# A block read by an adding transfer freed at a later slot, and a chunk's small factors moved down the order, in a three-layer cross-interaction kernel

## The chip, the cores and the metric

The kernel runs on one core of one Trainium2 chip. The metric is the device time of one launch in microseconds (us). The kernel before was timed in three runs; a fourth execution was profiled.

## The reference, cut to what matters

The input `r_x` has 1024 batch items, 64 features and 16 embedding columns, in f32. Three layers follow each other. Each multiplies all pairs of features of the input with the features of the running state, and contracts the pairs with a weight matrix of 128 rows:

```
x0 = h = x                                  # (1024, 64, 16)
for i in range(3):
    z = einsum('bfe,bge->bfge', x0, h)      # all pairs of features
    y = einsum('oc,bce->boe', W[i], z) + b[i]
    x_i, h = (y[:, :64], y[:, 64:]) if i < 2 else (y, y)
    xs.append(x_i)
out = sum(concatenate(xs, axis=1), axis=2) @ fc_w.T + fc_b     # (1024, 1)
```

Only one number per batch item leaves, so the kernel folds the last layer's weights and the output vector into the weights of the layers before, ahead of the main part.

## The kernel before, in words

**Tiling.** The 1024 items are cut into 32 chunks of 32 items; a chunk has 32 x 16 = 512 columns. The products of pairs of features of one chunk fill 16 tiles of 128 rows by 512 columns. Four tiles make a block (128 x 2048, f32, 1 MB), and the kernel keeps 14 such blocks (`blocks`, in the profile all `z`). A block of products is one VectorE instruction (L633, or L241 for the first and last chunks): the chunk's features (`xa`, loaded from HBM) times a quarter of its rotated features (`xb`, loaded from HBM and copied by ScalarE into a PSUM bank `xp`, L553).

**Blocks are handed out by a list.** `take` pops the block that has been free longest from the front of the list `vacant`, with a count of its uses. `used` lowers the count, and at zero the block goes to the end of the list. All this happens while the program is written, not on the chip; on the chip a new writer of a block waits with semaphores until the readers of its old contents are done. So the place in the written order at which `used` is called decides which block the next product gets, and with it what that product waits for.

**Pairs.** Chunks 2, 3, 0, 1 come first, with chunks 4 and 5 behind them; then 13 pairs of chunks (pair 3 with chunks 6 and 7, pair 4 with 8 and 9, up to pair 15), and the rest of chunks 2 and 3 at the end. A pair's two contractions are done with seven runs of matmuls in place of eight, on sums and differences of blocks. VectorE makes the products B22, T3, X and B21, each in two blocks numbered j = 0 and 1 (`make_pair`, L685). GpSimd mixes them (`w_mix`, L642): T2 = X - T3, T3 = B22 + T2, T2 = T2 + B21. For j = 1 T2 takes the place of X (from pair 4 on). The last mix for j = 1 is no GpSimd instruction: it is a DMA from block to block that adds (`accum_op=ALU.add`, L648), started from GpSimd's queue, reading B21[1] and adding it to T2[1].

**The order of the work** is written out by hand. `at(when, fn, ...)` puts a step into a list; the list is sorted by `when` and run. One unit of `when` is one slot, in which TensorE does one matmul for the first column of work and one for the second. A pair has a window of 31 slots (`SPAN`), `t = T0 + SPAN * n` with `T0 = 33`, and `window` (L731) fills the two columns with the matmul runs (all matmuls of the main part are issued by the helper at L525, each as two records). The window begins with four matmuls on X[1], and beside them four on T3[0]. Each engine runs its own instructions strictly in the order in which they were written.

**The names around the change.** The adding transfer of a pair is written at slot t + 17.6 for the first pair and t + 18.6 for the others. The matmuls that read B21[1] (the run `beta`) are written up to slot t + 19.5 in the first pair's window and t + 24.5 in the others. B21[1] has five uses, four matmuls and one mix. The product X[1] of the next pair is taken at slot t + 29 (`when[7]` = -2 against its own window's start). The `factors` of chunks 4 and 5 (L275) are for each chunk one ScalarE copy with a scale (L279) and one VectorE instruction on 64 rows (L286); `sums` (L291) is one VectorE reduction. They read the accumulators `acc` of chunks 4 and 5. `w_both` (L637) adds two quarters in a PSUM bank (L639), from which the product T3 is made.

Of the kernel before, what the change touches and what calls it, by code (L numbers as in the profile page):

```python
# [39 lines left out]
ALU = mybir.AluOpType  # L40
# [29 lines left out]
def cin_kernel(ctx, tc, xra, xrb, wh, w0r, w1h, w2t, wx1, wx0, vec, out):  # L70
    nc = tc.nc
# [8 lines left out]
    def const_tile(name, shape):  # L80
        return const.tile(shape, F32, tag=name, name=name)

    blocks = [const_tile(f"z{n}", [128, NI, N]) for n in range(NZ)]
    vacant, left = list(range(NZ)), {}

    def take(uses=1):
        n = vacant.pop(0)
        left[n] = uses
        return n

    def used(n, times=1):
        left[n] -= times
        assert left[n] >= 0
        if left[n] == 0:
            vacant.append(n)
# [272 lines left out]
    for h in range(2):  # L368
        at = slice(32 * h, 32 * h + 32)
# [145 lines left out]
    def at(when, fn, *args, **flags):  # L515
        ops.append((when, len(ops), fn, args, flags))
# [125 lines left out]
    def w_mix(p, j, out, in0, in1, first=0, last=NI):  # L642
        p.setdefault(out, {})
        if j not in p[out]:
            p[out][j] = p["X"][j] if j and p["k"] > 3 else take(9)
        o, x, y = p[out][j], p[in0][j], p[in1][j]
        if in1 == "B21" and j:
            nc.gpsimd.dma_start(out=blocks[o], in_=blocks[y], accum_op=ALU.add)  # L648
        else:
            nc.gpsimd.tensor_tensor(  # L650
                *(blocks[b][:, first:last] for b in (o, x, y)),
                ALU.subtract if in1 == "T3" else ALU.add,
            )
        if last < NI:
            return
        for b in (x, y):
            if b != o:
                used(b)
# [26 lines left out]
    def make_pair(t, p, when, mixed):  # L685
        a, b = p["a"], p["b"]
        for when, c, j, name, uses in (
            (when[0], b, 2, "B22", 5), (when[1], b, 0, None, 0), (when[2], b, 0, "T3", 9),
            (when[3], a, 0, "X", 5), (when[4], b, 3, "B22", 5), (when[5], b, 1, None, 0),
            (when[6], b, 1, "T3", 9), (when[7], a, 1, "X", 13 if p["k"] > 3 else 5), (when[8], a, 2, "B21", 5),  # L690
            (when[9], a, 3, "B21", 5),
        ):
            if name is None:
                at(t + when, w_both, p, j)
                continue
            if name == "B21" and j == 2 and p["k"] == 3:
                at(t + when, w_product, p, c, j, name, uses, engine=nc.gpsimd)
                continue
            if name != "T3":
                ahead = 3.3 if p["k"] > 4 and name == "B22" and j == 2 else 2.7  # L700
                if p["k"] == 3 and name == "X" and j == 1:
                    ahead = 9.1
                at(t + when - ahead, second, c, j)
            at(t + when, w_product, p, c, j, name, uses)
        t2, t1, t4 = ("T2", "X", "T3"), ("T3", "B22", "T2"), ("T2", "T2", "B21")
        for when, j, names in zip(
            mixed, (0, 1, 1, 0, 1, 1, 0), (t2, (*t2, 0, 2), (*t2, 2), t1, t1, t4, t4)
        ):
            at(t + when, w_mix, p, j, *names)

    def p4_run(p):
        return w_run(p, delta, wh_all, "T2", at_t=2 * NI)
# [82 lines left out]
    T0 = 33  # L795
# [27 lines left out]
    for c in (0, 1):  # L823
        at(34.5, factors, c)
    at(34.6, sums, 0, slice(0, 128), slice(0, 1))
    for c in (4, 5):
        at(T0 + 21, factors, c)
    at(T0 + 21.1, sums, 2, slice(0, 128), slice(0, 1))


    pairs = []
    for n in range(NPAIR):
        k = n + 3
        s = k % 2
        p = {
            "k": k, "A": halves[s], "O": halves[1 - s], "b": 2 * k + s, "a": 2 * k + 1 - s,
        }
        pairs.append(p)
        t = T0 + SPAN * n
        if n == 0:  # L840
            load_pair(t, p, -39.9, -33.3, -33.15, -27)
            make_pair(
                t, p, (-23.4, -20.7, -20.4, -17.8, -17.2, -16.8, -16.6, -7, -13.5, 3),
                (-14, -6.9, -6.8, 7.2, 12.4, 17.6, 17.5),
            )
            left5 = [[(contract_half, 5, 3, i, n) for i in (2, 3)] for n in range(2)]
            window(
                t, p, ([left5[1][0], (q_extra, 4, va)], [left5[1][1]]),
                [left5[0][0], (q_extra, 5, va), None, None], [left5[0][1], None],
                GROUPS,  # L850
            )
        else:
            q = pairs[-2]
            load_pair(t, p, -34, -28, -27.8, -27.7)
            make_pair(
                t, p, (-21.4, -18.7, -18.4, -15.8, -12.2, -9.5, -6.1, -2, 1.6, 4.2),
                (-5, 1.6, 3.6, 7.2, 12.4, 18.6, 18.5),
            )
            window(t, p, (first_fill(q), second_fill(q)), late_run(q))
            end_pair(t, q, (0.7, 11.7, 17.9, 22.3, 23.2, 24, 27.5))  # L860
# [40 lines left out]
    t, q = T0 + SPAN * NPAIR, pairs[-1]  # L901
    first, cuts = slice(0, CUT), (slice(0, E * CUT), slice(E * CUT, N))
# [93 lines left out]
    last = cuts[1]  # L996
# [84 lines left out]
```

## Time and profile before

| what | us |
|---|---|
| three timed runs | 463.65, 463.70, 465.69 |
| median of them | 463.70 |
| the profiled execution, its own time | 464.71 |
| its span in the profile | 462.9 |
| TensorE busy (2302 matmul records) | 448.8 |
| VectorE busy (284 instructions) | 393.6 |
| GpSimd busy (125 instructions) | 364.4 |
| ScalarE busy (215 instructions) | 116.7 |

The span is what the profile's clock covers, from 0 to 462.9; 1.8 us of the execution's own time lie outside it. Places in the span are given in us from its start. A matmul's record may overlap the next one's, so TensorE's busy time is an upper bound. "PEclk" is the clock granted to TensorE as a share of full speed. In the profile PE is TensorE, PEld its weight load, DVE is VectorE, ACT is ScalarE, POOL is GpSimd, and SP the engine that starts the loads. Pair 4, the second pair, is the one with chunks 8 and 9.

### The profile page before, as it was taken

What the parts mean: (1) busy time and instruction counts of PE and PEld (TensorE: products, weight loads), DVE (VectorE), ACT (ScalarE), POOL (GpSimd) and SP (SyncE); (2) the same over time, 40 slices, a digit from 0 to 9 for tenths busy, and PEclk for the clock granted to TensorE, in tenths of its full rate; (3) what the DMA queues carried; (4) which work ended last, traced back from release to release, by engine and by line L of the source; (5) the groups of instructions that cost most, each with busy time, mean ns of one, the idle gap of its engine ahead of it and who ended that gap; (6) DMA issues with size and microseconds to landing.
All of it is one profiled execution on the core that took longest, in us unless ns stands there. A gap on an engine that the chain in (4) does not pass through costs nothing.

```text
span 462.9 us, 6067 instructions
## 1 busy us (share of the span) xinstructions
PE 448.8 (97%) x2302; PEld 161.4 (35%) x2302; DVE 393.6 (85%) x284; ACT 116.7 (25%) x215; POOL 364.4 (79%) x125
## 2 busy tenths in 40 slices
PE   8999999995899999999999999999999999999897
PEld 4565343331233333333333323333333333333235
DVE  3995599984789899999989999999999899998643
ACT  2162341231131223131131223122131313124011
POOL 5424679996597989979797998979797998979800
PEclk9999999999799999999999999999999999999999
DMA  8995997496718759393967959394976949490500
GB/s 298 416 295 144 339 409 297 149 306 149 273 55 207 280 115 382 67 320 130 272 227 169 320 111 349 88 310 153 243 258 141 347 103 342 136 273 23 115 0 2
DMA packets 34484, 99.67 MB, mean 215 GB/s; under 512 B 6324, under 2 KB 6996, under 8 KB 27864
## 3 DMA queue, kind: packets, MB, share of 16 engines
q1 hardware_dynamic: 31800, 84.70, 50.7%
q0 software_dynamic: 1872, 13.63, 16.6%
q10 hardware_dynamic: 784, 0.95, 0.8%
q8 instruction: 18, 0.29, 0.3%
q14 instruction: 10, 0.08, 0.0%
HBM read 84.00 MB, written 1.64 MB: 185 GB/s over the span
## 4 chain that ended last, share of the span: by engine, by line
PE 78%; DVE 10%; DMA 5%; issue 5%; SPq 0%; POOL 0%; ACT 0%; POOLq 0%; DVEq 0%; ACTq 0%
PE alpha L525 48%; PE delta L525 8%; PE acc L525 6%; PE acc L251 6%; DVE z L633 5%; DMA z<-z 4%; PE q L525 3%; PE acc L269 3%; PE beta L525 2%; DMA z<-in_w0r 2%; DVE acc L293 1%; DVE uu L289 1%; DVE uu L681 1%; DVE delta L678 1%; DVE xp L639 1%
## 5 line engine op out<-in xcount | busy, mean ns | idle before, releaser
L650 POOL TENSOR_TENSOR z<-z,z 128x2048 f32<-128x2048 f32 (+1 forms) x78 | 299.7, 3871 | 38.3 <-PE alpha L525 38.0
L633 DVE TENSOR_TENSOR z<-xa,xp 128x2048 f32<-128x2048 f32 x103 | 232.4, 2280 | 10.5 <-DMA z<-z 8.0
L525 PE MATMUL alpha<-z,ws 128*64 128x512 f32 x624 | 219.1, 592 | 0.0
L525 PEld LDWEIGHTS alpha<-z,ws 128*64 128x64 f32 x624 | 69.1, 137 | 117.7 <-issue 116.6
L525 PE MATMUL alpha<-z,w_all 128*64 128x512 f32 x208 | 94.6, 609 | 6.6 <-DVE z L633 5.8
L525 PE MATMUL delta<-z,w_all 128*64 128x512 f32 x208 | 95.6, 593 | 2.7 <-DMA z<-z 2.2
L553 ACT COPY xp<-xb 128x512 f32<-128x512 f32 x88 | 51.6, 588 | 172.0 <-DVE z L633 139.6
L525 PE MATMUL delta<-z,ws 128*64 128x512 f32 x208 | 94.6, 609 | 0.0
L525 PE MATMUL beta<-z,w_all 128*64 128x512 f32 x208 | 91.7, 593 | 0.0
L525 PEld LDWEIGHTS alpha<-z,w_all 128*64 128x64 f32 x208 | 28.1, 140 | 71.8 <-issue 54.6
L241 DVE TENSOR_TENSOR z<-xa,xp 128x2048 f32<-128x2048 f32 (+2 forms) x23 | 45.1, 2003 | 7.0 <-ACT xp L553 5.3
L241 POOL TENSOR_TENSOR z<-xa,xb 128x2048 f32<-128x2048 f32 x6 | 27.5, 4637 | 19.9 <-DMA xb<-in_xrb 19.9
L525 PEld LDWEIGHTS delta<-z,w_all 128*64 128x64 f32 x208 | 28.3, 137 | 34.7 <-issue 30.2
L251 PE MATMUL acc<-z,w_all 128*64 128x256 f32 x256 | 29.0, 381 | 1.5 <-DVE z L241 1.3
L525 PE MATMUL acc<-z,w_all 128*64 128x512 f32 (+1 forms) x96 | 29.4, 594 | 0.0
L525 PEld LDWEIGHTS delta<-z,ws 128*64 128x64 f32 x208 | 28.1, 140 | 0.0
L525 PEld LDWEIGHTS beta<-z,w_all 128*64 128x64 f32 x208 | 27.8, 137 | 0.0
L251 PEld LDWEIGHTS acc<-z,w_all 128*64 128x64 f32 x256 | 18.1, 137 | 13.8 <-DVE z L241 2.9
L664 ACT ACTIVATE snap<-alpha,vs 64x512 f32<-64x512 f32 x13 | 8.9, 683 | 53.8 <-PE alpha L525 53.8
L661 ACT COPY snap<-alpha 64x512 f32<-64x512 f32 x13 | 7.6, 581 | 51.5 <-PE delta L525 51.5
L293 DVE TENSOR_REDUCE acc<-uu 128x64 f32<-128x1024 f32 (+2 forms) x19 | 19.6, 1036 | 0.2
L639 DVE TENSOR_TENSOR xp<-xp,xb 128x512 f32<-128x512 f32 x26 | 18.2, 699 | 0.8
(117 smaller groups left out, 350.5 us busy)
## 6 DMA issues: line engine op xcount, KB each, us to landing
xa<-in_xra SPq DMA_DIRECT2D x32, 1024.0 KB, 9.5
xb<-in_xrb SPq DMA_DIRECT2D x128, 256.0 KB, 7.8
z<-z POOLq DMA_DIRECT2D x13, 1024.0 KB, 9.1
e<-in_xra SPq DMA_DIRECT2D x28, 128.0 KB, 7.1
xx<-in_xra SPq DMA_DIRECT2D x28, 128.0 KB, 6.9
z<-in_w2t SPq DMA_DIRECT2D x2, 1024.0 KB
z<-in_wx SPq DMA_DIRECT2D x2, 1024.0 KB, 9.5
z<-in_w1h SPq DMA_DIRECT2D x1, 1024.0 KB
```

Source lines behind the costliest of these rows:

```text
L241: engine.tensor_tensor(blocks[zs[c, j]][:, at, :], xas[c][:, at, :], xbs[c][j].unsqueeze(1).to_broadcast([128, last - first, N]), ALU.mult,)
L251: nc.tensor.matmul(accs[c][halves[n]], w_all[:, t, 0:64], blocks[zs[c, j]][:, i, n * H2 : (n + 1) * H2], start=(t == 0), stop=(j == last a ...
L269: nc.tensor.matmul(accs[c][halves[1 - c % 2]], w_all[:, t, 64:128], blocks[zs[c, j]][:, i, :], start=(t == 0), stop=False, skip_group_chec ...
L289: nc.vector.scalar_tensor_tensor(uu[:, to, :], ys[k], cx, xxs[k], ALU.add, ALU.mult)
L293: nc.vector.tensor_reduce(acc[rows, of, k, half], uu[rows, of if at is None else at, E * half.start : E * half.stop].rearrange("p k (b e) ...
L525: nc.tensor.matmul(out, w, rhs, start=start, stop=stop, skip_group_check=True)
L553: nc.scalar.copy(bank, xbs[c][j])
L633: engine.tensor_tensor(blocks[b], xas[c], xbs[c][j].unsqueeze(1).to_broadcast([128, NI, N]), ALU.mult)
L639: nc.vector.tensor_tensor(bank, bank, xbs[p["b"]][j], ALU.add)
L650: nc.gpsimd.tensor_tensor(*(blocks[b][:, first:last] for b in (o, x, y)), ALU.subtract if in1 == "T3" else ALU.add,)
L661: nc.scalar.copy(snaps[0][p["O"]], alpha(p))
L664: nc.scalar.activation(snaps[1][p["O"]], alpha(p), AF.Identity, bias=bh1[p["A"]])
```

## The change

Two edits. In the first, `w_mix` no longer counts the adding transfer as a use of B21[1] where it is written; `make_pair` counts it at slot t + 29 of the pair's window. So B21[1] goes to the end of the list of free blocks at t + 29, where it went there with its last matmul before (t + 19.5 in the first pair, t + 24.5 in the others). In the second, the factors of chunks 4 and 5 and their sum move from slot T0 + 21 and T0 + 21.1 to T0 + 25.2, T0 + 25.3 and T0 + 25.4, which is behind `w_both` (T0 + 21.5) and the product T3[1] (T0 + 24.9) of pair 4.

```diff
         if in1 == "B21" and j:
             nc.gpsimd.dma_start(out=blocks[o], in_=blocks[y], accum_op=ALU.add)
-        else:
-            nc.gpsimd.tensor_tensor(
-                *(blocks[b][:, first:last] for b in (o, x, y)),
-                ALU.subtract if in1 == "T3" else ALU.add,
-            )
+            return
+        nc.gpsimd.tensor_tensor(
+            *(blocks[b][:, first:last] for b in (o, x, y)),
+            ALU.subtract if in1 == "T3" else ALU.add,
+        )
         if last < NI:
             return
         for b in (x, y):
...
             at(t + when, w_mix, p, j, *names)
+        at(t + 29, lambda: used(p["B21"][1]))
...
-    for c in (4, 5):
-        at(T0 + 21, factors, c)
-    at(T0 + 21.1, sums, 2, slice(0, 128), slice(0, 1))
+    for c, when in ((4, 25.2), (5, 25.3)):
+        at(T0 + when, factors, c)
+    at(T0 + 25.4, sums, 2, slice(0, 128), slice(0, 1))
```

## The prediction, on record before the changed kernel ran

> **What bounds the kernel now.** I read the shares by engine first, then busy time by stage, then the waits, and last the chain and the timelines around the stage that falls out of line. The page, then the busy times cut at the starts of the pairs' windows (columns: stretch, its length, busy us and instructions of PE, PEld, DVE, ACT, POOL, granted clock, DMA share, GB/s):
>
> ```profile
> PE 448.8 (97%) x2302; PEld 161.4 (35%) x2302; DVE 393.6 (85%) x284; ACT 116.7 (25%) x215; POOL 364.4 (79%) x125
> PEclk9999999999799999999999999999999999999999
> ```
>
> ```profile
> 111.40:117.30 5.90, 0.10 (x4) 0.00 (x0) 2.30 (x2) 0.01 (x1) 0.81 (x1) 0.87 0.95 260
> 117.30:146.10 28.80, 28.77 (x125) 8.94 (x126) 24.34 (x18) 6.33 (x12) 23.59 (x7) 0.91 0.54 151
> 146.10:172.40 26.30, 26.15 (x126) 8.47 (x126) 24.50 (x18) 6.39 (x12) 23.60 (x7) 1.00 0.69 217
> 172.40:198.60 26.20, 26.19 (x126) 8.50 (x128) 24.46 (x18) 6.37 (x12) 23.62 (x7) 1.00 0.72 222
> ```
>
> TensorE bounds nearly everything: a pair takes 26.2 us with TensorE busy all but about 0.1. VectorE (24.5 of 26.2) and GpSimd (23.6) follow. Two rows are out of line, both at pair 4: 5.9 us with TensorE empty ahead of its window, and a window of 28.8 us instead of 26.2, with a clock of 0.91. Who is waited for (us in total, times, longest):
>
> ```profile
> PE alpha L525 <- DVE z L633: 5.8, 1, 5.8
> DVE z L633 <- DMA z<-z: 8.0, 6, 5.0
> ```
>
> The chain of work in that stretch, then VectorE's and TensorE's own timelines (start, us, what, and idle time before it):
>
> ```profile
> 106.67 8.17 DMA z<-z
> ...
> 114.97 2.30 DVE z L633
> ...
> 117.31 1.11 PE alpha L525
> ```
>
> ```profile
> 103.08 0.74 DVE L286 SCALAR_TENSOR_TENSOR uu<-acc,vs,snap 64x512 f32<-64x512 f32 x1 [1.02 <-ACT snap L279]
> 105.36 0.76 DVE L286 SCALAR_TENSOR_TENSOR uu<-acc,vs,snap 64x512 f32<-64x512 f32 x1 [1.54 <-ACT snap L279]
> 106.15 0.69 DVE L293 TENSOR_REDUCE acc<-uu 128x32 f32<-128x512 f32 x1
> 106.87 0.70 DVE L639 TENSOR_TENSOR xp<-xp,xb 128x512 f32<-128x512 f32 x1
> 107.67 2.29 DVE L633 TENSOR_TENSOR z<-xa,xp 128x2048 f32<-128x2048 f32 x1
> 114.97 2.29 DVE L633 TENSOR_TENSOR z<-xa,xp 128x2048 f32<-128x2048 f32 x1 [5.00 <-DMA z<-z]
> ```
>
> ```profile
> 110.90 0.59 PE L525 MATMUL y<-e,v 64*64 64x512 f32 x2
> 117.31 1.11 PE L525 MATMUL alpha<-z,w_all 128*64 128x512 f32 x1 [5.81 <-DVE z L633]
> ...
> 121.63 1.06 PE L525 MATMUL alpha<-z,w_all 128*64 128x512 f32 x1
> 122.48 0.68 PE L525 MATMUL alpha<-z,w_all 128*64 128x512 f32 x1
> 123.00 0.59 PE L525 MATMUL alpha<-z,w_all 128*64 128x512 f32 x1
> ```
>
> The reader is to see one story. The product at 114.97 is X[1] of pair 4, with which TensorE's next window begins. VectorE was free from 109.97, and the copy X[1] needs was made at 105.35. X[1] waited because its block is that of pair 3's B21[1], which the adding transfer was still reading (106.67 to 114.87). TensorE had ended pair 3 by about 111.4. Its matmuls then step by 0.85 us until 122.48, against 0.43 in every other window.
>
> **What the Trainium skill says.** "TensorE: Matmul & The Clock Gate", Part 1 (the HAM clock gate): an idle window of some 3.4 us sets TensorE to half clock, and about as long a busy one sets it back, with a phase that varies from run to run. The trace agrees: after 5.8 us of idling, half rate for 5.2 us. "DMA: Bandwidth & Descriptors", Issuing engines are not separate DMA queues: transfers of all queues run on the same 16 engines and interleave. So the adding transfer and SP's loads can slow each other. In the trace the 13 adding transfers land in 8.2 to 10.2 us (median 9.1), most of them beside loads.
>
> **Part 1, the later release.** No instruction is added or taken away. With both programs' instruction lists side by side, X[1] of pair 4 now gets the block of chunk 5's last products, whose last matmul started at 104.05, and its wait for the transfer is gone. It is then free to run once VectorE gets there. Alone, this edit would start X[1] at 109.97 and end it at 112.3, some 0.9 after TensorE is ready.
>
> The wait on the transfer moves to T3[0] of the pair after next in order (pair 5's T3[0] waits for pair 3's transfer, and so on 10 more times, and at the end one product of chunk 3). Behind T3[0] on VectorE stand X[0] and B22[1] of the same pair, and TensorE's next window waits for them. In the regular windows the transfer starts about 20.2 us into a window (166.28 in that from 146.09) and lands at most 10.2 later, 4.2 into the next; T3[0] starts 9.4 into its window (155.53). So 5 us are spare, and T3[0] is held up only by a transfer of over 9.4 + 26.2 - 20.2 = 15.4 us: cost 0. The waits this takes off B21[1] in later pairs (3.0 us in five places) gain nothing: TensorE is busy 26.1 of 26.2 us there.
>
> Other blocks also move one place down the list. The nearest reader I find is for B21[1], which now gets the block of T3[1], read last some 25 us into the former window (by 144.9 where the next begins at 146.09), while B21[1] starts 2.9 us into the next (149.0): 4 us spare, cost 0.
>
> **Part 2, the factors.** ScalarE's order stays as it is. On VectorE, `w_both` (0.70) and T3[1] (2.29) go ahead of two L286 (0.74 and 0.76) and one L293 (0.69). VectorE ended B22[1] at 102.05. Then `w_both` runs from 102.1 to 102.8 and T3[1] to 105.1; their inputs are there (loads issued by 91.3 land in at most 8.0; T3[1]'s block was last read by GpSimd's mix ending about 93.3). The factors need ScalarE's copies, made by 103.04 and 105.33: 105.1 to 105.85 and 105.85 to 106.6. The sum ends at 107.3, and X[1] runs from 107.35 to 109.65 (its copy was ready at 105.94). The 1.02 and 1.54 us in which VectorE waited for ScalarE are filled. If ScalarE's second copy came later, X[1] would move with it; 1.7 us are spare before 111.4. Pair 4's accumulators take the PSUM banks of chunks 4 and 5; these are read by 106.6, also in time.
>
> T3[1] ends 4.9 us sooner, so on SP's queue the load of `xa` for chunk 10, which waited for it (issued at 109.99), and six `xb` loads behind it (110.42 to 115.5) go out from about 105.1. They are not needed before X[0] of pair 5, about 123.
>
> **Sum.** TensorE starts pair 4's window at 111.4 rather than 117.31: 5.9 us. Without an idle window the clock stays full, and the window takes 26.2 rather than 28.8: 2.6 us. Together 8.5.
>
> **What is late next.** GpSimd's first half of T2[1] waits for the window's second matmul on X[1]: in regular windows it starts 2.0 in (148.11 against 146.09), so at 113.4; GpSimd was free at 112.2. VectorE's next step after X[1] waits for TensorE's last matmuls of pair 3 (111.5), and from there runs as in a regular window. Pair 3's own T2[1] is read in slot 9, 7.7 us in, so at 119.1; its transfer lands at 114.9, but now runs beside the loads sent out earlier. In all 1.0 + 1.5 MB of loads and 1 MB of transfer; at the 260 GB/s of the crowded stretch 13.5 us from 105.1, so 118.6 at worst. Bounds: 0 to 1 us of stall. I take 0, since in the regular windows loads go out 3.3 us behind the transfer (142.74 against 139.49) and it still lands in 8 to 10 us.
>
> The profiled execution's 464.71 less 8.5 is 456.2. The median, 463.70, lies 1.0 lower. Whether that 1.0 is in the ramp of the clock, which goes, or around it, which stays, the profile can't say: 455.2 to 456.2, and I take the middle, **455.7**.
>
> **Rivals.**
> 1. *The forecast*: 454.2 to 456.9, 0.82.
> 2. *A new wait in the stall's place*, at window 4: the transfer is slowed by the earlier loads past 119.1, or X[1] comes after 111.4. For: the crowded stretch shows a DMA share of 0.95. Against: the 4 us of margin worked out above. With 2 to 4 us of stall, 457.5 to 459.5; 0.10.
> 3. *The edit doesn't do what it says*: X[1] ends up waiting for something else as late as 114.9, such as a reader of its new block. For: the list is short, so that each block is used again soon. Against: that reader ended at 104.65. About 463.7; 0.03.
> 4. *Slower*: T3[0] becomes the product that waits for a transfer, in 11 pairs, and delays X[0], B22[1] and TensorE behind it. It decides from the point at which a transfer takes 15.4 us and the 1 us that VectorE idles ahead of L681 in a regular window (0.94 at 160.95): 16.4. At 17.4 it would cost 1 us a pair, 11 in all, so 463.7 - 8 + 11 = 467. For: VectorE has only 1.7 us of slack per pair. Against: the longest of 13 transfers took 10.2. 0.05.
>
> Range 454.0 to 458.2: the forecast with its two ends, and the milder part of rival 2. What a measurement of this kernel can tell from no change is about 0.5%, 2.3 us. Faster by more than that 0.92, within it 0.03, slower 0.05.
>
> **What would show it.** Right: no TensorE gap near 111 longer than 0.5 us, PEclk 9 in the slice with the 7, window 4 of 26.2 us, X[1] ending near 109.7 after the two L286, no VectorE wait for the transfer anywhere. Wrong: a gap of several us at window 4 under another name (a weight load or `delta` waiting for the transfer near 119), T3[0] waiting for a transfer in later pairs, or a period above 26.2.

## The result, and the profile after

Four runs of the changed kernel gave 456.65, 456.77, 458.11 and 458.23 us, median 457.44, against a median of 464.59 in four of the kernel before (463.65 to 465.69). The ratio is 0.9845 with a 95% interval of 0.9809 to 0.9882: 7.2 us less, inside the range. The median is 1.7 above the forecast of 455.7; 0.9 of these lie in the kernel before, which the forecast took from three runs (463.70) and which has 464.59 in four. The profiled execution took 458.11 with a span of 456.3, which is 6.6 less than before in both.

The granted clock by slice (from the page), then the stretches around pair 4's window, in the columns explained above:

```profile
PEclk9999999999999999999999999999999999999899
```

```profile
111.40:117.30 5.90, 5.90 (x32) 1.93 (x30) 5.52 (x4) 0.59 (x1) 4.69 (x3) 1.00 1.08 276
117.30:137.70 20.40, 20.40 (x100) 6.49 (x96) 18.77 (x14) 5.14 (x9) 20.02 (x6) 1.00 0.61 182
```

The empty stretch from 111.4 to 117.3 is full, at a clock of 1.00, and the next window begins at 137.81 where it began at 146.09. But the row of clocks holds an 8 in a place where there was a 9 before, near the end. VectorE's and TensorE's timelines at pair 4:

```profile
102.31 0.70 DVE L639 TENSOR_TENSOR xp<-xp,xb 128x512 f32<-128x512 f32 x1
103.14 2.29 DVE L633 TENSOR_TENSOR z<-xa,xp 128x2048 f32<-128x2048 f32 x1
105.34 1.53 DVE L286 SCALAR_TENSOR_TENSOR uu<-acc,vs,snap 64x512 f32<-64x512 f32 x2
106.91 0.69 DVE L293 TENSOR_REDUCE acc<-uu 128x32 f32<-128x512 f32 x1
107.62 2.29 DVE L633 TENSOR_TENSOR z<-xa,xp 128x2048 f32<-128x2048 f32 x1
111.75 0.76 DVE L671 SCALAR_TENSOR_TENSOR snap<-alpha,vs,snap 64x512 f32<-64x512 f32 x1 [1.84 <-PE y L525]
```

```profile
111.13 0.59 PE L525 MATMUL y<-e,v 64*64 64x512 f32 x2
111.66 0.64 PE L525 MATMUL alpha<-z,w_all 128*64 128x512 f32 x1
112.14 0.59 PE L525 MATMUL alpha<-z,w_all 128*64 128x512 f32 x1
...
137.81 0.64 PE L525 MATMUL alpha<-z,w_all 128*64 128x512 f32 x1
```

X[1] runs at 107.62, behind the sum of the factors, and ends at 109.91. It is VectorE that now waits for TensorE (1.84 us). Window 4 starts at 111.66 with no wait, and its matmuls step by 0.48 and then 0.43 us. The last line is the start of the next window.

The end is where the two profiles part again. The fences show TensorE's first matmul that reads the last pair's T2[1], which waits for the last adding transfer, the matmuls of its run two and three steps on, and a later matmul on `hx`; first the kernel before, then the changed one:

```profile
437.57 0.64 PE L525 MATMUL delta<-z,w_all 128*64 128x512 f32 x1 [2.21 <-DMA z<-z]
...
438.48 0.59 PE L525 MATMUL delta<-z,w_all 128*64 128x512 f32 x1
...
438.90 0.59 PE L525 MATMUL delta<-z,w_all 128*64 128x512 f32 x1
...
445.01 0.64 PE L525 MATMUL hx<-e,vs 64*64 64x512 f32 x1
```

```profile
429.34 1.11 PE L525 MATMUL delta<-z,w_all 128*64 128x512 f32 x1 [2.27 <-DMA z<-z]
...
431.10 1.06 PE L525 MATMUL delta<-z,w_all 128*64 128x512 f32 x1
...
431.95 0.96 PE L525 MATMUL delta<-z,w_all 128*64 128x512 f32 x1
...
438.42 0.64 PE L525 MATMUL hx<-e,vs 64*64 64x512 f32 x1
```

Both kernels wait here, 2.21 and 2.27 us. In this profile the changed one comes out of the wait at half clock, which lasts to about 432.7. That splits the 6.6 us between the profiles: 8.2 us are ahead at this matmul (437.57 less 429.34), and 6.6 are left at the matmul on `hx` behind it (445.01 before, 438.42 after). So 1.6 us were given back in one place.

### The profile page after: what moved, and what is told of

Same layout as the page of the kernel before. It is cut to its first block, busy times and chain, and to the rows that moved or that the text cites. A ratio compares the mean times of both kernels' runs of the same rounds, so it can differ in the third digit from the quotient of the medians.

```text
span 456.3 us, 6069 instructions
## 1 busy us (share of the span) xinstructions
PE 447.7 (98%) x2302; PEld 161.6 (35%) x2302; DVE 392.8 (86%) x284; ACT 116.5 (26%) x215; POOL 364.4 (80%) x125
## 3 DMA queue, kind: packets, MB, share of 16 engines
q0 software_dynamic: 1872, 13.63, 16.6%
## 4 chain that ended last, share of the span: by engine, by line
PE 80%; DVE 10%; issue 4%; DMA 4%; POOL 1%; SPq 0%; ACT 0%; POOLq 0%; ACTq 0%
PE alpha L525 48%; PE delta L525 9%; PE acc L525 6%; PE acc L251 6%; DVE z L633 5%; PE q L525 3%; PE acc L269 3%; PE beta L525 3%; DMA z<-z 2%; DMA z<-in_w0r 2%; DVE acc L293 1%; POOL z L650 1%; DVE uu L289 1%; DVE uu L681 1%; DVE delta L678 1%
## 5 line engine op out<-in xcount | busy, mean ns | idle before, releaser
L525 PE MATMUL delta<-z,w_all 128*64 128x512 f32 x208 | 97.2, 601 | 3.4 <-DMA z<-z 2.3
L525 PE MATMUL alpha<-z,w_all 128*64 128x512 f32 x208 | 92.0, 595 | 0.8
L525 PE MATMUL delta<-z,ws 128*64 128x512 f32 x208 | 92.0, 595 | 0.0
L681 DVE SCALAR_TENSOR_TENSOR uu<-alpha,snap 64x512 f32<-64x512 f32 x13 | 9.0, 689 | 12.1 <-PE alpha L525 12.1
```

The costliest lines, as they stand in the source:

```text
L525: nc.tensor.matmul(out, w, rhs, start=start, stop=stop, skip_group_check=True)
L681: nc.vector.scalar_tensor_tensor(uu[p[out], 0], x(p), 1.0 / QS, factor[p[out]], ALU.mult, ALU.mult)
```

## The experiments

**The theory** after the result: the whole gain is at pair 4, by the later release; the move of the factors fills idle time of VectorE and is worth at most 1 us. What is missing from the 8.5 us is clock lost in the gap at the end. **Rivals**: the move carries the gain; the later pairs' waits count; the half clock has no price of its own. Each run below was timed beside the kernel before on its own chip, and the ratio is to that.

| run | median us | ratio to before | 95% interval |
|---|---|---|---|
| changed kernel, again | 457.41 | 0.9860 | 0.9833 to 0.9887 |
| later release alone | 457.56 | 0.9841 | 0.9816 to 0.9866 |
| factors moved alone | 468.58 | 1.0080 | 1.0057 to 1.0104 |
| later release for pair 3 alone | 457.35 | 0.9849 | 0.9819 to 0.9879 |
| before, gap filled with 12 matmuls | 465.22 | 1.0009 | 0.9997 to 1.0022 |
| before, gap filled with 6 | 462.63 | 0.9958 | 0.9941 to 0.9975 |
| changed, end gap filled with 4 | 457.55 | 0.9861 | 0.9834 to 0.9888 |
| changed, end gap filled with 2 | 456.03 | 0.9829 | 0.9804 to 0.9853 |
| last mix on GpSimd | 453.05 | 0.9767 | 0.9737 to 0.9798 |
| the same, again | 453.30 | 0.9764 | 0.9739 to 0.9788 |
| last mix on GpSimd, old factors | 454.42 | 0.9791 | 0.9767 to 0.9815 |
| the same, again | 453.97 | 0.9776 | 0.9754 to 0.9799 |

**The later release alone.** The changed kernel with the factors put back:

```diff
-    for c, when in ((4, 25.2), (5, 25.3)):
-        at(T0 + when, factors, c)
-    at(T0 + 25.4, sums, 2, slice(0, 128), slice(0, 1))
+    for c in (4, 5):
+        at(T0 + 21, factors, c)
+    at(T0 + 21.1, sums, 2, slice(0, 128), slice(0, 1))
```

> The later release alone, the factors where they were before. My theory: X[1] of pair 4 follows T3[1] at once, starts at about 110.2 and ends at 112.5, TensorE starts window 4 at 112.55 instead of 111.66, so 0.9 us is lost against the changed kernel and nothing else: about 0.9 above it, 457.6 to 459.1 where the changed kernel has 456.7 to 458.2. SP's loads go out from 110 again, so pair 3's adding transfer lands in 8 to 9 us, not in 12.3. Rival (the factors carry the gain): the gap ahead of window 4 stays over 3 us and the time is above 461.

457.56, no different from the changed kernel. TensorE waits for X[1], but less than the 0.9 us expected. VectorE's two products T3[1] and X[1] back to back, and TensorE's start of window 4:

```profile
107.22 4.49 DVE L633 TENSOR_TENSOR z<-xa,xp 128x2048 f32<-128x2048 f32 x2
```

```profile
111.76 0.64 PE L525 MATMUL alpha<-z,w_all 128*64 128x512 f32 x1 [0.48 <-DVE z L633]
```

The idle time is 0.48. The transfers landed in 8.1 to 9.8 us here, against up to 12.3 in the changed kernel, as expected. The release carries the gain, as far as these times can tell; the rival falls.

**The factors moved alone**, the same lines of the diff put into the kernel before.

> The factors moved alone, the release where it was before. X[1] of pair 4 waits for the adding transfer again. My theory: since T3[1] now ends near 105.4, SP's loads go out from 105.5 and slow the transfer to some 12.3 us, as in the changed kernel's trace; it lands near 119.2, X[1] ends near 121.6, the gap ahead of window 4 grows from 5.8 to about 10 us, and the kernel is slower than before by 4 us: about 468.5. Rival (order on VectorE alone counts): no change, X[1] waits to about 115 as before, 463.7 to 465.7. Second rival: faster by about 1.

468.58, as the theory had it, and slower than before beyond its interval. The waits of VectorE, then the two products and TensorE:

```profile
DVE z L633 <- DMA z<-z: 16.3, 8, 11.3
```

```profile
102.04 2.29 DVE L633 TENSOR_TENSOR z<-xa,xp 128x2048 f32<-128x2048 f32 x1
...
118.19 2.29 DVE L633 TENSOR_TENSOR z<-xa,xp 128x2048 f32<-128x2048 f32 x1 [11.29 <-DMA z<-z]
```

```profile
120.53 1.12 PE L525 MATMUL alpha<-z,w_all 128*64 128x512 f32 x1 [9.69 <-DVE z L633]
```

```profile
104.36 0.33 SPq L145 DMA_DIRECT2D xa<-in_xra  x1
104.79 3.10 SPq L159 DMA_DIRECT2D xb<-in_xrb  x6
```

T3[1] is 5.6 us earlier than before, so the seven loads (2.5 MB, the last fence: SP's queue) go out from 104.36, just ahead of the transfer issued at 105.80, which lands after 12.3 us instead of 8.2. X[1] waits 11.3 us for it. With the block freed too early, finishing sooner on VectorE makes the kernel slower. The same 12.3 us are in the changed kernel, where the transfer landed at 119.2; it cost 0.6 us of a weight load's wait and no gap in the matmuls, since T2[1] is read only at 119.43.

**The later release for pair 3 alone**, the block of the other twelve pairs freed as before:

```diff
             nc.gpsimd.dma_start(out=blocks[o], in_=blocks[y], accum_op=ALU.add)
+            if p["k"] > 3:
+                used(y)
             return
...
-        at(t + 29, lambda: used(p["B21"][1]))
+        if p["k"] == 3:
+            at(t + 29, lambda: used(p["B21"][1]))
```

> The changed kernel with the later release for the first pair (pair 3) alone; in the other twelve pairs the block is freed as before. My theory: the whole gain is at pair 4, so the time equals the changed kernel's, 456.7 to 458.2, and VectorE shows the short waits for the transfer in later pairs again (up to 3 us in all) without an effect on TensorE. Rival (the later pairs' waits counted): slower than the changed kernel by 1 to 3 us, 458.5 to 461.

457.35. VectorE waits for adding transfers five times again, and the median is the changed kernel's:

```profile
DVE z L633 <- DMA z<-z: 3.1, 5, 1.0
```

Two of the six runs, 459.27 and 459.68, fall in the rival's range, but their clock was 0.993 where the other four have 0.996 or 1.000. A gain in the later pairs doesn't show.

**The gap of the kernel before, filled.** Matmuls on the weights, whose results nothing uses, keep TensorE busy while X[1] waits (6 in place of 12 in the second run). They are extra work.

```diff
+    wide = w_all[:, 0:4, :].rearrange("p t g -> p (t g)")
+    def keep_busy(bank, n):
+        for _ in range(n):
+            mm(bank(), w_all[:, 0], wide, start=True, stop=True)
+    at(T0 + 30.9, keep_busy, lambda: w_bank(pairs[1], "alpha", "acc", 4), 12)
```

> The kernel before with twelve extra matmuls (128 x 512, about 5.2 us) put into TensorE's empty stretch ahead of pair 4's window; they write a PSUM bank whose contents the window then starts anew, so the output is the same. My theory: the stall of 5.9 us stays, but TensorE is not idle long enough for its clock to be halved; window 4 takes 26.2 instead of 28.8 us and the time falls by 2.6 to about 462.0, its granted clock in that window 1.00. Rival (the clock is lowered by the wait itself or by the load, not by idling): window 4 stays at 28.8 and the time at 463.7 to 465.7.

465.22, no gain. The clock was 1.000 in all 14 runs, but the edit was mis-sized:

```profile
112.14 10.57 PE L525 MATMUL alpha<-w_all 128*128 128x512 f32 x24
122.64 0.64 PE L525 MATMUL alpha<-z,w_all 128*64 128x512 f32 x1
```

The 12 (24 records) took 10.5 us, not 5.2, and held window 4 up to 122.64, 4.4 us past the end of X[1] at 118.28. What the clock gave, they took. The expectation that comes next has 9.3 and 3 us, which leave out the last three of these records. So half as many:

> The kernel before with six extra matmuls in the gap ahead of pair 4's window, half as many as in the run before this: twelve took 9.3 us where I had reckoned 5.2, and ran 3 us past the point at which X[1] was ready. Six should take some 4.7 us and end inside the gap. My theory: the wait stays, the clock in window 4 is 1.00 and the window 26.2 us; 2.6 us less than before, about 462. Rival (the halved clock costs nothing that is not lost elsewhere): no change, 464 to 465.

462.63, 2.0 us below before (interval 1.2 to 2.7). The fillers, window 4's start, and the window's row:

```profile
112.67 5.42 PE L525 MATMUL alpha<-w_all 128*128 128x512 f32 x12
118.50 0.64 PE L525 MATMUL alpha<-z,w_all 128*64 128x512 f32 x1 [0.42 <-DVE z L633]
```

```profile
116.80:143.00 26.20, 25.78 (x117) 8.46 (x118) 24.40 (x18) 6.32 (x11) 22.48 (x7) 1.00 0.53 169
```

The wait for X[1] is still there, and the matmuls behind it run at full clock: the next transfer is issued 20.2 us into the window (138.69), as in a regular one, where before it was 22.2 (139.49 against 117.31). The window after it starts at 144.65, so this one took 26.15 us, and the half clock has a price of its own, apart from the wait. The size of the gain is less certain: in this trace the gap at the end is also shorter, 1.50 us in place of 2.21, and 13 of the 22 runs had a clock below 1.000 (0.996 in 11, 0.993 in 2); where these lost it isn't on record.

**The end gap of the changed kernel.** First the changed kernel once more, then with 4 and with 2 filling matmuls (`keep_busy` as above) ahead of the first one that reads the last T2[1]:

```diff
+    at(t + 0.6, keep_busy, lambda: ps.tile([128, N], F32, tag="y", name="idle"), 4)
```

> The changed kernel once more, for comparison on the same chip. My theory: its times fall in two groups 1.6 us apart, near 456.7 and near 458.2, by whether the clock is halved after the gap of 2.3 us near the end (429.34), where TensorE waits for the last pair's adding transfer. Rival: one group, scattered evenly.

The times were 456.32, 457.22, 457.34, 457.48, 457.61 and 458.61: not two groups. The mean granted clock was 0.996 in four runs and 1.000 in two (456.32 and 457.61). 0.004 of 455.6 us is 1.8 us, so the clock is lost in some runs and not in others, but what is left of the scatter, over 1 us, is as large. This run's trace (gap 2.45 us) and those of the release alone (2.25) and of pair 3 alone (2.27), all at 0.996, have the half clock at the same place and about as long. But there it begins only 0.5 to 0.9 us after the matmuls have started again, as in the run with the release alone:

```profile
429.42 0.64 PE L525 MATMUL delta<-z,w_all 128*64 128x512 f32 x1 [2.25 <-DMA z<-z]
429.90 0.99 PE L525 MATMUL delta<-z,w_all 128*64 128x512 f32 x1
```

> The changed kernel with four extra matmuls (128 x 512, about 1.7 us) in TensorE's gap near the end, ahead of the first matmul that reads the last pair's T2[1]; they write a PSUM bank that nothing reads. My theory: the wait for the last transfer stays, the clock is never halved there, the two groups of times become one, near 456.7, within 0.4. Rival (the two groups come from elsewhere, such as the start): times near 456.7 and near 458.2 as before.

457.55: no gain. The 4 took 3.7 us in a gap of 2.3 and held the next matmuls up. The clock was 1.000 in five runs and 0.996 in one (458.62). Half as many:

> The changed kernel with two extra matmuls in the gap near the end, half as many as in the run before this: four took 3.7 us in a gap of 2.3 and held the next matmuls up by 1.2. Two should take 1.8. My theory: no window of halved clock (granted clock 1.00 in every run), and the upper times (458 and over, clock 0.996) go: 455.9 to 457.4, median 456.7. Rival (the scatter is not from the clock): times from 456.3 to 458.6 as in the changed kernel.

456.03, with a clock of 1.000 in all five runs (455.19 to 457.5). The gap is down to 0.33:

```profile
426.55 1.98 PE L525 MATMUL idle<-w_all 128*128 128x512 f32 x4
428.87 0.64 PE L525 MATMUL delta<-z,w_all 128*64 128x512 f32 x1 [0.33 <-DMA z<-z]
```

The loss of clock is gone, which the theory needs. The gain of about 1.4 us in the median is between two chips, and the intervals of the two ratios overlap, so its size is not shown.

**A version that beats both.** This is the changed kernel with the last pair's mix done as an addition on GpSimd instead of a transfer, so that T2[1] is ready sooner:

```diff
-        if in1 == "B21" and j:
+        if in1 == "B21" and j and p["k"] < NPAIR + 2:
             nc.gpsimd.dma_start(out=blocks[o], in_=blocks[y], accum_op=ALU.add)
             return
...
-        if last < NI:
+        if last < NI or in1 == "B21" and j:
             return
```

> The changed kernel with the last pair's adding transfer replaced by a GpSimd addition, as for j = 0; the other twelve stay transfers. My theory: T2[1] is ready 4.6 us after GpSimd gets to it (near 424.9) instead of 9.2 (429.3), ahead of TensorE's need at 427; the gap of 2.3 us goes and with it the halved clock; GpSimd's two last products come 4.6 us later, ending near 434.7, and are read only after 440. So 454.5, in one group. Rival: those two products or another wait take the gap's place (456.7 or more).

453.05, and 453.30 when it was run again, 11 us below before, and below the 454.5 expected. Eleven of these twelve runs have a clock of 1.000, and one has 0.996 (454.69). GpSimd's timeline, then TensorE around the place of the gap:

```profile
402.58 22.77 POOL L650 TENSOR_TENSOR z<-z,z 128x1024 f32<-128x1024 f32 x6 [2.52 <-PE alpha L525]
425.30 9.04 POOL L241 TENSOR_TENSOR z<-xa,xb 128x2048 f32<-128x2048 f32 x2
```

```profile
427.11 0.59 PE L525 MATMUL beta<-e,va 128*64 128x512 f32 x1
427.54 0.59 PE L525 MATMUL delta<-z,w_all 128*64 128x512 f32 x1
```

GpSimd is done with the addition at about 425.3, ahead of the matmul at 427.54, which follows without a gap. The two products behind it end at 434.3 and nobody waits for them.

**What the factors' move is worth**, on that version, whose times scatter less (last mix on GpSimd, factors at their old place), on two chips:

> The changed kernel with the last pair's adding transfer done on GpSimd, and with the factors of chunks 4 and 5 back at their old place. My theory: the factors' move is worth at most the 0.5 us that TensorE waits for X[1] in the run with the release alone, which a measurement can't tell from nothing: 453.0 to 453.6. Rival (the move carries part of the gain): 454 or more.

> The version with the last mix on GpSimd and the factors at their new place once more, beside the one with the old place, on one chip; the two were apart by 0.24% of the kernel before's time on two chips, with overlapping intervals. My theory: 0 to 0.5 us faster than the one with the old place. Rival (the move counts): over 1 us faster.

> The version with the last mix on GpSimd and the factors at their old place once more. My theory: 0 to 0.5 us above the one with the new place. Rival: over 1 us above.

454.42 is in the rival's range, but the version with the new place (453.05) had run on another chip. Side by side on one chip they have 453.97 with the old place and 453.30 with the new. That is 0.7 us between medians, between the theory's 0.5 and the rival's 1, with overlapping intervals. TensorE's start of window 4 in the two traces with the old place:

```profile
112.14 0.64 PE L525 MATMUL alpha<-z,w_all 128*64 128x512 f32 x1 [0.47 <-DVE z L633]
112.11 0.64 PE L525 MATMUL alpha<-z,w_all 128*64 128x512 f32 x1 [1.41 <-DVE z L633]
```

X[1] ends near 112.1 in both. TensorE ended pair 3 at different times: in the first trace it had waited 0.74 us for GpSimd's mix ahead of that, in the second not at all. With the new place it doesn't wait for X[1] in either trace. So the move saves TensorE 0.5 to 1.4 us of waiting, more than the theory's bound in one of two traces; a gain in the time is not shown clear of the noise.

## Why the prediction was right, and where it was off

- **What bounds it, and part 1: right.** The block that was still being read was the cause, at one place. Without the wait TensorE started window 4 at 111.66 (foretold 111.4). The release alone gives the gain, and released late for pair 3 alone it gives all of it. The price set for the release without the move, 0.9 us, was 0.48, 0.47 and 1.41 in the three traces that have it: GpSimd's mix ended at another time in each, and with it pair 3, whose end I had taken from one profile.
- **The clock in window 4: right.** 2.6 us were foretold; the next window began 26.15 us after 111.66, against 28.8 before, and filling the gap of the kernel before gave 2.0 us (1.2 to 2.7) with the wait still there. This is the clock gate of the Trainium skill ("TensorE: Matmul & The Clock Gate", Part 1), and the trace agrees: with the idle stretch of 5.8 us gone, window 4 had a clock of 1.00.
- **Part 2: right on the path, wrong in what I called its cover.** VectorE's order came out within 0.3 us of the steps worked out. For the earlier loads I wrote "118.6 at worst" and took 0; the transfer landed at 119.2, past the bound, with 0.2 us left before T2[1] was read. The bound was summed short: a block has 1.05 MB (13.63 MB for 13 transfers on the page), so loads and transfer are 3.67 MB, which at 260 GB/s take 14.1 us from 105.1, to 119.2, past the read that I had put at 119.1. The 4 us of margin set against rival 2 took the transfer as undisturbed. The cost was 0 as foretold, but by luck: the reason given (8 to 10 us beside loads in the regular windows) does not hold when the loads go out ahead of the transfer, when it took 12.3.
- **The moved wait on T3[0]: right.** The changed kernel's trace shows no wait of VectorE for an adding transfer.
- **The term that was off: the sum's end.** At the start of the next window 8.3 of the 8.5 us were there, at the last gap 8.2. I let the rest of the run stand as in the profile of before, which happened to pass the last gap of 2.21 us at full clock. The changed kernel's passed 2.27 us and lost 1.6. Its clock was 0.996 in seven of its ten runs. With the two variants that leave this gap open (release alone, pair 3 alone) 7 of 22 runs have 1.000; where the gap is filled or gone, in six of the table's rows, 30 of 32 have it. The kernel before has the gap too, and of its 68 runs beside the experiments 52 show 0.993, as its profile does, and 15 one step less, 0.989. If that step is the end's, it is lost less often there; no trace shows it. The measured 7.2 us (interval 5.5 to 8.9) does not exclude 8.5. The half of an unexplained 1.0 us that the forecast took off for three runs found no support in the fourth: with it the median of before, 464.59, is close to the profiled 464.71.

## What to carry to other kernels

Where blocks are handed out in order of release, count a transfer as a reader until it has landed; a block freed where the transfer is written may come up again while it is still being read, for the one product that the next stage begins with. Price a stall of TensorE with the slow clock behind it, and look for gaps left elsewhere that may or may not trip it. An earlier step can release loads that slow a transfer that a later step waits for, so try the halves of a change apart: here one half gave the gain as far as the times can tell, and the other alone made the kernel slower.

## What the runs showed of the hardware that was not expected

- The 1 MB adding transfers took 7.8 to 10.2 us in the six profiles with the factors at their old place. In each of the eight with the new place, where the first pair's transfer is issued 1.0 to 1.5 us behind the first of its loads, the slowest took 12.0 to 12.6; in the two looked at closely (changed kernel, factors alone) it is that transfer. The same addition on GpSimd takes about 4.6.
- Gaps of 2.25, 2.27, 2.27 and 2.45 us were each followed by some 3.4 us of half clock in four traces, at once or within 0.9 us of the restart; gaps of 2.21 and 2.23 us at the same place (the kernel before, the factors alone) were not. A threshold between them isn't shown, since only one run of each kernel has a trace. The Trainium skill ("TensorE: Matmul & The Clock Gate", Part 1) speaks of an idle window of some 3.4 us, free-running; why a shorter gap suffices isn't shown here. Filled to 0.33 us, the clock was 1.000 in five of five runs.
